# A decoder layer on one core: the stage of cross values and feed-forward in another order

## Chip, core and metric

The kernel runs on one core of a Trainium2 chip. The metric is the device time of one execution in microseconds (us). Engines are named as in the profile: PE (TensorE), DVE (VectorE), ACT (ScalarE), POOL (GpSimd), SP (the queue that issues the DMAs). Each engine works through its own instructions in the order in which the program issued them; an instruction that waits holds back everything queued behind it on its engine.

## What is computed

One decoder layer over 8 sequences of 128 tokens and 512 features, in float32. Three blocks follow each other; each adds to x, and a layernorm (no gain, no bias) follows each:

```python
x = _layernorm(x + attn(x))            # causal self-attention, 32 heads, 4-bit weights
x = _layernorm(x + xattn(x, ctx, ctx)) # cross-attention, 16 heads of 32
x = _layernorm(x + ffn(x))
```

In the cross-attention the softmax runs over the axis of sequence and head, not over the keys (`softmax(scores, axis=0)` with scores of shape (8*16, 128, 128)). So each weight needs the sum over all sequences, and each sequence's exponentials can only be weighed at the end. The feed-forward is

```python
h = relu(layernorm(xf @ gw1.T + gb1) * gamma + beta)   # gate, 32 wide
gates = h @ gw2.T + gb2                                # 8 experts, top 2
main = xf @ weight.T                                   # 512 x 512
tmp = einsum('ni,eir->enr', xf, lora_A)                # 8 x 16, weighed by the gate
out = main + einsum('enr,ero->no', tmp * w, lora_B) / 16
```

with a limit on how many tokens an expert may take over all 1024 tokens, so that the expert part is finished only when all tokens have passed the gate.

## The kernel before

The first 620 us or so are the self-attention, the cross projections and the cross scores. Then comes the stage that the change touches, a loop over the sequences i = 0 to 7 in which TensorE works on three sequences at once. What one round issues, and in which order, is written out by hand in a string, `AV_SEQ` (L62); each letter is one step (`step`, L1294), and letters without a meaning do nothing:

- A, `cross_values(i)` (L1251): 16 heads times (values x weighed exponentials), 32 matmuls into the bank "sc", copied by ACT to `avs`.
- B, `cross_residual(i)` (L1268): four transposes of `avs` on PE (tr_av), DVE adds them to the residual `acc`, then `normalised` (L214): bn_stats and bn_aggr on DVE, then three small operations on POOL (the add of epsilon, L199; the power, L200; the negated mean times that, L211).
- L: ACT applies the normalisation of sequence i-1 in place (L218).
- X, `turn_x2(i-1)` (L1090): four transposes of the normalised x (tr_x), copied by ACT to `x2f`.
- P, `gate_in(i-1)` (L1095): x times the gate's first layer and lora_A together (pg, 160 columns), ACT copies the lora part to `tmp` (L1099), DVE adds gb1 to make `h` (L1101), then `normalised` for h, as above.
- N: ACT applies the oldest waiting normalisation of h (L218).
- f: the next quarter of the main product of sequence i-2 (L1111): one 128x512 float32 product, which the trace shows as two matmuls. Up to four are waiting per round; what the letters don't take is issued at the round's end.
- W: one of four weighings (`weigh`, L1080): exponentials of four heads times the inverse sum, 128x512, in place. By `WEIGH_ON = 'vvgg'` the first two of a round run on DVE, the others on POOL.
- E (rounds 5, 6, 7): ACT moves a finished main product from its bank to `acc`.
- G, H, h in round 5 and J, K in round 7: the gate's second layer. G and J transpose h of several sequences and ACT applies relu (L1122, L1123); H and K multiply by gw2 (pgate, L1130); h is one of two halves of the top-2 choice on DVE (L1141 on), 11 small operations. The first group (sequences 0 to 3) has its transposes and pgate in the bank "tr", which X uses too; the second (4, 5) in "sc", which A uses.

At the start of round 4 thirteen memsets and two small POOL operations, and three small ones on DVE, prepare tables for the gate (L1324 to L1338). Before the loop the exponentials of sequences 0 and 1 are weighed (L1217 to L1224); in the loop, round i weighs sequence i+1. After the loop a second string, `END_SEQ`, orders the rest: the four quarters for sequence 6, then X for sequence 7, and everything up to the output.

Of the kernel before, what the change touches and what calls it, by code (L numbers as in the profile page):

```python
# [10 lines left out]
F32 = mybir.dt.float32  # L11
# [4 lines left out]
ALU = mybir.AluOpType  # L16
# [3 lines left out]
P = 128  # L20
B, S, D = 8, 128, 512
# [12 lines left out]
EPS = 1e-5  # L34
# [24 lines left out]
WEIGH1_ON = 'vvgg'  # L59
LADD_AT = 4  # L60
GSUM_ON = 'g'
AV_SEQ = 'LNEvvWWfvfAvWXJWffBdfKPGdffHhfffhff'  # L62
GATES = ((0, 4, 'tr'), (4, 2, 'sc'), (6, 1, 'po'), (7, 1, 'tr'))
GATE_IN = 5
LATE_SOFT = 6
# [75 lines left out]
def decoder_kernel(ctx: ExitStack, tc: tile.TileContext, a: dict, out: bass.AP):  # L141
    nc = tc.nc

    const = ctx.enter_context(tc.tile_pool(name="const", bufs=1))
    stat = ctx.enter_context(tc.tile_pool(name="stat", bufs=4))
# [25 lines left out]
    minus_half = const.tile([P, 1], F32, name="minus_half")  # L171
# [15 lines left out]
    def statistics(x, name, wait=0, aggregations=None):  # L187

        st = stat.tile([P, 6], F32, tag="bn", name=f"bn_{name}")
        nc.vector.bn_stats(st[:], x)  # L190
        mv = stat.tile([P, 2], F32, tag="mv", name=f"mv_{name}")
        if aggregations is None:
            nc.vector.bn_aggr(mv[:], st[:])
        else:
            aggregations.append(lambda: nc.vector.bn_aggr(mv[:], st[:]))
        rstd = stat.tile([P, 1], F32, tag="rstd", name=f"rstd_{name}")

        def power():
            nc.gpsimd.tensor_scalar(rstd[:], mv[:, 1:2], EPS, None, ALU.add)  # L199
            nc.gpsimd.tensor_tensor(rstd[:], rstd[:], minus_half[:], ALU.pow)  # L200

        if aggregations is None:
            later(wait, power)
        else:
            aggregations.append(power)
        return mv, rstd

    def negated(mv, rstd, name):

        nmr = stat.tile([P, 1], F32, tag="nmr", name=f"nmr_{name}")  # L210
        nc.gpsimd.tensor_scalar(nmr[:], mv[:, 0:1], rstd[:], -1.0, ALU.mult, ALU.mult)  # L211
        return nmr

    def normalised(x, name):  # L214

        mv, rstd = statistics(x, name)
        nmr = negated(mv, rstd, name)
        return lambda: nc.scalar.activation(x, x, AF.Identity, scale=rstd[:], bias=nmr[:])  # L218

    def layernorm(dst, t, tag, wait=0):  # L220
# [8 lines left out]
    def later(n, f, projects=False):  # L229

        if slot[0] == 0 or n == 0:
            return f()
        delayed.append((slot[0] + n, f, projects))
# [609 lines left out]
    def chunk(hf, m, rg):  # L843
        return (hf * KT + m) * 4 + rg
# [28 lines left out]
    def group_of(c):  # L873
        return next(i for i in range(GROUPS) if c < FIRST[i + 1])

    def max_of(gi):
        return gmax[:, gi, :] if gi < EARLY else lmax[:, gi - EARLY + 1, :]
# [20 lines left out]
    def across(x, n=HALF):  # L898
        return x.unsqueeze(1).to_broadcast([P, n, S])
# [180 lines left out]
    def weigh(b, m, engine):  # L1080
        hf, j = divmod(b, HALF)
        c, end = chunk(hf, m, 0), chunk(hf, m, 0) + 4
        while c < end:
            gi = group_of(c)
            n = min(end, FIRST[gi + 1]) - c
            e = quads[c // 4][:, c % 4 : c % 4 + n, j, :]
            engine.tensor_tensor(e, e, across(max_of(gi), n), ALU.mult)  # L1087
            c += n

    def turn_x2(t):  # L1090
        tr = transposed(bank("tr", f"tr_x2{t}", (P, KT, S)), t)
        x2f[t] = fp.tile([P, KT, S], F32, tag="x2f", name=f"x2f{t}", bufs=3)
        nc.scalar.copy(x2f[t][:], tr[:])

    def gate_in(t):  # L1095
        ps = bank("av", f"pg{t}", (P, FW - D))
        for kt in range(KT):
            nc.tensor.matmul(ps[:], x2f[t][:, kt, :], fg[:, kt, :], start=(kt == 0), stop=(kt == KT - 1))
        nc.scalar.copy(tmp[:, t, :], ps[:, :P])  # L1099
        ht = h[:, t, :]  # L1100
        nc.vector.tensor_tensor(ht, ps[:, P:], rows["gb1"][:], ALU.add)  # L1101
        return normalised(ht, f"g{t}")
# [112 lines left out]
    def engine_of(m, on=WEIGH_ON):  # L1215
        return nc.vector if on[m] == "v" else nc.gpsimd
# [34 lines left out]
    def cross_values(i):  # L1251

        av = bank("sc", f"xav{i}", (P, KT, S))
        hf, j = divmod(i, HALF)
        for k in range(XH):
            m, g = divmod(k, 4)
            nc.tensor.matmul(
                av[ts(g, XD), m, :],
                values_of(i)[:, ts(k, XD)],
                scores_of(chunk(hf, m, g))[:, j, :],  # L1260
                start=True,
                stop=True,
                tile_position=(0, g * XD),
            )
        avs[i] = fwp.tile([P, KT, S], F32, tag="raw", name=f"avs{i}", bufs=KT)
        nc.scalar.copy(avs[i][:], av[:])

    def cross_residual(i):  # L1268
        tr = bank("po", f"tr_av{i}", (P, KT, S))
        for m in range(KT):  # L1270
            nc.tensor.transpose(tr[:, m, :], avs[i][:, m, :], ident[:])
        res = acc[:, i, :].rearrange("p (d h) -> p d h", h=XH)
        nc.vector.tensor_tensor(
            res, res, tr[:].rearrange("p m (g d) -> p d m g", g=4).rearrange("p d m g -> p d (m g)"), ALU.add
        )
        apply[i] = normalised(acc[:, i, :], f"x{i}")

    def evacuate(t):
        if EVACUATE_ON == "a":
            nc.scalar.copy(acc[:, t, :], outp.pop(t)[:])  # L1280
        else:
            nc.vector.tensor_copy(acc[:, t, :], outp.pop(t)[:])

    def gate(k, what):

        t, n, tag = GATES[k]
        if what == "G":
            gate_turn(t, n, tag)
        elif what == "H":
            pg[k] = gate_top(t, n, gate_out(t, n, tag))  # L1290
        else:
            pg[k].pop(0)()

    def step(what, i, state):  # L1294
        if what == "L" and i - 1 in apply:
            apply.pop(i - 1)()
        elif what == "W" and 0 < i + 1 < B and i:
            m = state["w"] = state.get("w", -1) + 1
            weigh(i + 1, m, engine_of(m))
        elif what == "A" and i < B:  # L1300
            cross_values(i)
        elif what == "B" and i < B:
            cross_residual(i)
        elif what == "X" and i:
            turn_x2(i - 1)
        elif what == "P" and i:
            norm[i - 1] = gate_in(i - 1)
        elif what == "N" and norm:
            norm.pop(min(norm))()
        elif what in "GHh" and i == GATE_IN:  # L1310
            gate(0, what)
        elif what in "JK" and i == B - 1:
            gate(1, "GH"["JK".index(what)])
        elif what == "E" and i in EVACUATE:
            evacuate(EVACUATE.index(i))
        elif what == "f" and fill:
            fill.pop(0)()

    for i in range(B):
        if i == 0:  # L1320
            f_cm = open_ffn()
        if i == GATE_IN - 1:
            for e in range(NE):
                nc.gpsimd.memset(rank[:, e : e + 1], float(NE - e))  # L1324
            nc.gpsimd.memset(ones[:], 1.0)
            nc.gpsimd.memset(minus_one[:], -1.0)
            for k in range(TOPK):
                nc.gpsimd.memset(orders[1][:, k, :], float(k))

            nc.vector.tensor_reduce(  # L1330
                experts[:, 0], ident[:].rearrange("p (e r) -> p e r", r=R), AX.X, ALU.add
            )
            nc.gpsimd.tensor_scalar(experts[:, 1], experts[:, 0], ALPHA, None, ALU.mult)
            nc.gpsimd.tensor_copy(experts[:, 0], experts[:, 1])
            of, other = (rank[:].unsqueeze(i).to_broadcast([P, NE, NE]) for i in (2, 1))
            nc.vector.tensor_tensor(orders[0][:, :, 0, :], other, of, ALU.is_lt)
            nc.vector.tensor_tensor(orders[0][:, :, 1, :], other, of, ALU.is_gt)
            nc.gpsimd.memset(hT[GH : GH + 1], 1.0)  # L1338
        state = {}
        for what in AV_SEQ:  # L1340
            step(what, i, state)
        while fill:
            fill.pop(0)()
        if i:
            fill.extend(main_product(i - 1, "proj"))
# [256 lines left out]
```

## Time and profile before

| | |
|---|---|
| median of 3 runs | 737.8 us (736.91 to 738.52) |
| profiled execution | 737.73 us |
| its span, first to last instruction | 735.9 us |
| mean granted PE clock over the span | 0.976 |
| loop of this stage, B of sequence 0 to X of sequence 7 | 639.70 to 702.66 us |

The profiled execution lies 1.83 us above its span and 0.07 us below the median. Rows of the timeline read: start, duration (both us), engine, line, operation, output<-input, shape, count; in brackets the idle time just ahead of it and who ended it. Starts of PE's transposes in the loop, by sequence:

| sequence | B (tr_av) | X (tr_x) |
|---|---|---|
| 0 | 639.70 | 645.82 |
| 1 | 646.73 | 652.62 |
| 2 | 654.83 | 659.90 |
| 3 | 662.12 | 666.76 |
| 4 | 668.97 | 675.50 |
| 5 | 679.32 | 686.31 |
| 6 | 688.52 | 693.16 |
| 7 | 696.97 | 702.66 |

### The profile page before, as it was taken

The page shows a single profiled execution, that of the slowest core. Times are in us where ns is not written, and L with a number is a line of the kernel's source. Part 1 is how long each engine was busy: PE and PEld are TensorE (multiplying, and loading weights), DVE is VectorE, ACT ScalarE, POOL GpSimd, SP SyncE. Part 2 cuts the span into 40 slices and gives each one's busy share as a digit, 9 for nine tenths or more (in the row PEclk, how much of TensorE's full clock was granted, in tenths as well). Part 3 has the DMA queues.
Part 4 walks back from the last instruction along what each step waited for, and adds up shares of the span by engine and source line. Part 5 has one row for each costly group of instructions (what it writes and reads, how often), then busy time and mean ns, then how long its engine had stood idle before and what let it go on. Part 6 is the DMA issues. An engine that isn't in the chain of part 4 may idle for free. (4 is left out here: it accounts for less than half of the span.)

```text
span 735.9 us, 12053 instructions
## 1 busy us (share of the span) xinstructions
PE 687.3 (93%) x3762; PEld 545.7 (74%) x3762; DVE 622.2 (85%) x1448; ACT 376.1 (51%) x1018; POOL 443.9 (60%) x434
## 2 busy tenths in 40 slices
PE   7899999999999999999999999999999898488875
PEld 4687788888888888888888888877887666355542
DVE  5989999999999999999999999998444989934555
ACT  4465655555565555465465554547524554132433
POOL 3764756667576775766758666577503566377325
PEclk9999999999999999999999999999999999689987
DMA  8778342443443343343343332163001001100003
GB/s 285 213 198 254 102 110 69 129 106 82 122 122 87 87 121 96 85 128 103 87 108 73 82 88 61 30 185 115 1 1 29 1 1 60 32 1 1 1 1 114
DMA packets 36242, 65.73 MB, mean 89 GB/s; under 512 B 5327, under 2 KB 7503, under 8 KB 36178
## 3 DMA queue, kind: packets, MB, share of 16 engines
q1 hardware_dynamic: 36178, 64.96, 32.0%
q8 instruction: 30, 0.49, 0.3%
q14 instruction: 34, 0.28, 0.1%
HBM read 41.87 MB, written 2.10 MB: 60 GB/s over the span
## 5 line engine op out<-in xcount | busy, mean ns | idle before, releaser
L392 ACT ACTIVATE p<-p,nmx 128x128 f32<-128x128 f32 x256 | 99.8, 391 | 88.8 <-DVE nmx L383 88.8
L310 PE MATMUL ps<-xh,w 128*128 128x512 f32 x336 | 140.8, 419 | 0.4 <-DVE part L320 0.4
L310 PE MATMUL ps<-xl,w 128*128 128x512 f32 x336 | 132.0, 393 | 0.0
L399 POOL TENSOR_TENSOR p<-p,rden 128x512 f32<-128x512 f32 x64 | 68.1, 1064 | 102.6 <-DVE rden L398 79.3
L320 DVE SCALAR_TENSOR_TENSOR part<-ps,scales,part 128x512 f32<-128x512 f32 x168 | 124.8, 743 | 2.0 <-PE ps L310 0.4
L344 POOL TENSOR_TENSOR sw<-sw,tables 128x512 f32<-128x512 f32 x71 | 92.7, 1306 | 50.4 <-DMA sw<-x 34.7
L345 POOL TENSOR_TENSOR q<-t,sw 128x512 f32<-128x512 f32 x62 | 93.6, 1510 | 10.0 <-DVE sw L344 5.0
L343 DVE TENSOR_TENSOR t<-x,tables 128x512 f32<-128x512 f32 x80 | 78.4, 980 | 0.7 <-POOL q L345 0.7
L378 PEld LDWEIGHTS sc<-k,q 128*128 128x128 f32 x512 | 67.0, 191 | 8.4 <-DVE q L345 2.1
L435 PE MATMUL po<-woh,ch 128*128 128x512 f32 x256 | 72.2, 403 | 0.0
L316 ACT ACTIVATE part<-ps,scales 128x512 f32<-128x512 f32 x84 | 57.8, 689 | 28.0 <-PE ps L310 28.0
L310 PEld LDWEIGHTS ps<-xh,w 128*128 128x128 f32 x336 | 63.3, 188 | 11.3 <-DVE part L320 0.6
L310 PEld LDWEIGHTS ps<-xl,w 128*128 128x128 f32 x336 | 63.7, 190 | 10.3
L378 PE MATMUL sc<-k,q 128*128 128x128 f32 x512 | 68.2, 275 | 2.5 <-DVE q L345 1.9
L435 PE MATMUL po<-woh,cl 128*128 128x512 f32 x256 | 69.4, 393 | 0.0
L435 PE MATMUL po<-wol,ch 128*128 128x512 f32 x256 | 69.4, 393 | 0.0
L184 ACT CAST ph<-tr 128x512 fp32r<-128x512 f32 x64 | 37.4, 584 | 53.7 <-PE tr L409 53.5
L383 DVE CUSTOM_DVE_ANT_0 p<-sc,causal 128x128 f32<-128x128 f32 x256 | 58.4, 283 | 0.3 <-PE sc L378 0.3
L320 DVE SCALAR_TENSOR_TENSOR x<-ps,scales,part 128x512 f32<-128x512 f32 x70 | 52.4, 749 | 5.5 <-PE ps L310 0.5
L435 PEld LDWEIGHTS po<-wol,ch 128*128 128x128 f32 x256 | 48.2, 188 | 10.9
L435 PEld LDWEIGHTS po<-woh,cl 128*128 128x128 f32 x256 | 48.1, 188 | 10.8
L435 PEld LDWEIGHTS po<-woh,ch 128*128 128x128 f32 x256 | 45.8, 189 | 8.4
(259 smaller groups left out, 1475.8 us busy)
## 6 DMA issues: line engine op xcount, KB each, us to landing
sw<-x SPq DMA_DIRECT2D x160, 128.0 KB, 2.3
raw<-in_qkv SPq DMA_DIRECT2D x28, 384.0 KB, 3.6
oraw<-in_qw_o SPq DMA_DIRECT2D x32, 256.0 KB, 2.8
osc<-in_scales_o SPq DMA_DIRECT2D x32, 256.0 KB, 3.7
xraw<-in_xT SPq DMA_DIRECT2D x4, 512.0 KB, 5.8
acc<-in_x SPq DMA_DIRECT2D x8, 256.0 KB, 5.4
ctxraw<-in_ctxT SPq DMA_DIRECT2D x2, 1024.0 KB, 7.1
out<-o SPq DMA_DIRECT2D x8, 256.0 KB, 2.0
```

Source lines behind the costliest of these rows:

```text
L184: nc.scalar.copy(hi, src)
L310: nc.tensor.matmul(ps[:], w[:, kt, ts(j, HD)], x[:, kt, ts(hf, HN)], start=(i == 0), stop=(i == 1))
L316: nc.scalar.activation(p[:], ps[:], AF.Copy, scale=sc)
L320: nc.vector.scalar_tensor_tensor(to, ps[:], sc, parts[0][:], ALU.mult, ALU.add)
L343: later(delay("cos"), lambda: engine("cos").tensor_tensor(seqs(t[:]), seqs(x[:]), table(cos_t[m]), ALU.mult), True)
L344: later(delay("sin"), lambda: engine("sin").tensor_tensor(seqs(sw[:]), seqs(sw[:]), table(sin_t[m]), ALU.mult), True)
L345: later(delay("q"), lambda: engine("q").tensor_tensor(dst, t[:], sw[:], ALU.add), True)
L378: nc.tensor.matmul(sc[:, r, :], t["q"][:, r, ts(j, S)], t["k"][:, ts(j, S)], start=True, stop=True)
L383: nc.vector.tensor_tensor_reduce(out=p[:, r, :], in0=sc[:, r, :], in1=causal[:], scale=-1.0, scalar=3e38, op0=ALU.add, op1=ALU.min, accum_ ...
L392: nc.scalar.activation(p[:, r, :], p[:, r, :], AF.Exp, scale=-1.0, bias=nmx[:, r : r + 1], accum_out=den[:, r : r + 1],)
L399: nc.gpsimd.tensor_tensor(p[:], p[:], rden[:].unsqueeze(2).to_broadcast([P, REP, S]), ALU.mult)
L435: nc.tensor.matmul(po[0][:], c[:, r, :], w[:, r, :], start=(r == 0 and i == 0), stop=(r == REP - 1 and i == 2))
```

## The change

Three edits. The order string is rewritten; a round weighs the sequence two ahead (rounds 0 to 5) instead of one ahead (rounds 1 to 6); and `normalised` does the add of epsilon on DVE instead of POOL.

```diff
-AV_SEQ = 'LNEvvWWfvfAvWXJWffBdfKPGdffHhfffhff'
+AV_SEQ = 'LENAXJfBWWfKffPWWGHhh'
...
     def normalised(x, name):
 
-        mv, rstd = statistics(x, name)
-        nmr = negated(mv, rstd, name)
+        st = stat.tile([P, 6], F32, tag="bn", name=f"bn_{name}")
+        nc.vector.bn_stats(st[:], x)
+        mv = stat.tile([P, 2], F32, tag="mv", name=f"mv_{name}")
+        nc.vector.bn_aggr(mv[:], st[:])
+        rstd = stat.tile([P, 1], F32, tag="rstd", name=f"rstd_{name}")
+        nc.vector.tensor_scalar(rstd[:], mv[:, 1:2], EPS, None, ALU.add)
+        nc.gpsimd.tensor_tensor(rstd[:], rstd[:], minus_half[:], ALU.pow)
+        nmr = stat.tile([P, 1], F32, tag="nmr", name=f"nmr_{name}")
+        nc.gpsimd.tensor_scalar(nmr[:], mv[:, 0:1], rstd[:], -1.0, ALU.mult, ALU.mult)
         return lambda: nc.scalar.activation(x, x, AF.Identity, scale=rstd[:], bias=nmr[:])
...
-        elif what == "W" and 0 < i + 1 < B and i:
+        elif what == "W" and i + 2 < B:
             m = state["w"] = state.get("w", -1) + 1
-            weigh(i + 1, m, engine_of(m))
+            weigh(i + 2, m, engine_of(m))
```

Without the letters that do nothing, and with f where four are waiting, a round on PE changes from

```
f f A(i) X(i-1) f f B(i) P(i-1)      main product of i-2
```

to

```
A(i) X(i-1) f B(i) f f f P(i-1)      main product of i-2
```

On DVE a round was: weighing pair, residual and statistics of x(i), h and its statistics. It becomes: residual and statistics of x(i), weighing pair, h and its statistics. On POOL the weighing pair moves from the round's start to its end, behind the operations of both statistics. On ACT the copy of `tmp` in a round keeps its place ahead of the next round's L; E moves ahead of N; N stays ahead of the copies of `avs` and `x2f`. In round 7, K (pgate of sequences 4 and 5) stays behind B and comes ahead of the last two f and P. DMAs and their order are the same.

More of the change, by code (lines that the diff above doesn't have):

```diff
@@ L206, in statistics, with normalised @@
         return mv, rstd
-    def negated(mv, rstd, name):
+    def normalised(x, name):
+        st = stat.tile([P, 6], F32, tag="bn", name=f"bn_{name}")
[5 more added lines that the diff above has]
+        nc.gpsimd.tensor_tensor(rstd[:], rstd[:], minus_half[:], ALU.pow)
         nmr = stat.tile([P, 1], F32, tag="nmr", name=f"nmr_{name}")
         nc.gpsimd.tensor_scalar(nmr[:], mv[:, 0:1], rstd[:], -1.0, ALU.mult, ALU.mult)
-        return nmr
-    def normalised(x, name):
-        mv, rstd = statistics(x, name)
-        nmr = negated(mv, rstd, name)
         return lambda: nc.scalar.activation(x, x, AF.Identity, scale=rstd[:], bias=nmr[:])
```

## The prediction

> **What bounds the kernel now.** I read the page first, then the waits of the stage from 625 to 700 us, then its timeline engine by engine, because the changed order only exists there: up to 640 us the two orders issue the same work, and from the last transposes of x (702.66 us) they do so again.
>
> ```profile
> PE 687.3 (93%) x3762; PEld 545.7 (74%) x3762; DVE 622.2 (85%) x1448; ACT 376.1 (51%) x1018; POOL 443.9 (60%) x434
> PEclk9999999999999999999999999999999999689987
> ```
>
> PE is busy 93% of the whole span, but the last slices, this stage, are its weakest, and there its clock is not full. The stage's waits (who, for whom, us in total, times, longest):
>
> ```profile
> ACT acc L218 <- POOL nmr_x L211: 17.5, 7, 5.3
> PE tr_x L819 <- ACT acc L218: 6.4, 6, 2.9
> PE xav L1257 <- DVE E L1087: 5.9, 2, 4.6
> ACT h L218 <- POOL nmr_g L211: 3.0, 6, 0.5
> ```
>
> PE waits for a weighing (DVE E) only twice, both for sequence 0, which neither order moves. What PE waits for later is the layernorm of x: six times, 6.4 us. The timeline of PE over one undisturbed round, and the one disturbed round:
>
> ```profile
> 659.90 0.66 PE L819 MATMUL tr_x<-ident,acc 128*128 128x128 f32 x4 [0.66 <-ACT acc L218]
> 660.40 1.88 PE L1111 MATMUL pf<-fw,x2f 128*128 128x512 f32 x4
> 662.12 0.60 PE L1271 MATMUL tr_av<-ident,avs 128*128 128x128 f32 x4
> 662.55 1.25 PE L1098 MATMUL pg<-fg,x2f 128*128 128x160 f32 x8
> 663.64 1.88 PE L1111 MATMUL pf<-fw,x2f 128*128 128x512 f32 x4
> 665.45 1.08 PE L1257 MATMUL xav<-E,xv 128*32 128x128 f32 x32
> ...
> 675.50 0.66 PE L819 MATMUL tr_x<-ident,acc 128*128 128x128 f32 x4 [2.11 <-ACT acc L218]
> 676.00 3.54 PE L1111 MATMUL pf<-fw,x2f 128*128 128x512 f32 x4
> ```
>
> Start to start, a round costs PE: X (tr_x) 0.50, one f (two matmuls, half of a pf row) 0.86, B (tr_av) 0.43, P (pg) 1.09, A (xav) 1.08; with four f 6.54 us. The rounds took 7.29 and 6.85 us (B at 654.83, 662.12, 668.97). The last row ran at half clock after PE had stood for 2.11 us. On ACT:
>
> ```profile
> 659.04 0.81 ACT L218 ACTIVATE acc<-acc,nmr_x,rstd_x 128x512 f32<-128x512 f32 x1 [2.21 <-POOL nmr_x L211]
> 660.36 0.41 ACT L218 ACTIVATE h<-h,nmr_g,rstd_g 128x32 f32<-128x32 f32 x1 [0.51 <-POOL nmr_g L211]
> 660.68 0.56 ACT L1266 COPY avs<-xav 128x512 f32<-128x512 f32 x1
> 661.15 0.59 ACT L1093 COPY x2f<-tr_x 128x512 f32<-128x512 f32 x1
> ```
>
> N (the gate's normalisation, row two) stands ahead of the copy of avs that B needs. Today it costs 0.51 us of ACT and no PE time: B comes at 662.12, over 0.8 us after that copy.
>
> **What the change does.** [...] No matmul, transpose, copy or DMA is added; SP's queue is untouched.
>
> *The loop through x becomes shorter.* B(i), residual, statistics, normalise, X(i), then B(i+1) after one f instead of two: 0.86 us less.
>
> *The add of epsilon goes from POOL (0.22) to DVE* (nearest row: the 128x6 add at L1198, 0.17). Sixteen times 0.17 on DVE; each chain gains about 0.1 us (POOL's add to its power 0.31 us; DVE's add follows the aggregate by 0.21, the power that by about 0.31 instead of 0.30). From below: nothing gained, if DVE is late.
>
> *The weighing pair on DVE moves* to just behind the statistics of x, the POOL pair behind those of the gate. DVE's pair now runs against POOL's power and nmr of the same x. The row that shows this price: nmr_x at 658.17 took 0.83 us beside the DVE pair of 657.61 to 658.87, and 0.27 at 665.59 without. The Trainium skill (SBUF — State Buffer, "Who interferes with whom") says that a DVE instruction with two SBUF inputs and a GpSimd instruction that reads SBUF lock each other out for the whole instruction, whichever is first. The trace agrees for POOL; but DVE's pair took 1.26 us although POOL's power was already running at 657.50, so I charge POOL alone. By the rule DVE's pair would start up to 0.6 us later, which matters in two rounds (gate statistics queued behind the pair): at most +1.2 us. I take 0.
>
> *P comes after all four f, and that is the new danger.* The gate statistics start 2.58 us later relative to B than now, but N keeps its place ahead of the avs copy. From B(i) to B(i+1) through the gate, each step with a row: B 0.43; three f 2.58; P to its copy tmp 1.29 (655.27 to 656.56); to h on DVE 0.30; to bn 0.22; to aggregate 0.30; to the new add 0.21; to POOL's power 0.31; to nmr 0.67; to N on ACT 0.30; to the avs copy 0.32; to B(i+1) 0.64 (639.06 to 639.70). Sum 7.57 us. Through x it is: tmp stands ahead of x's normalise on ACT, so that begins at 0.43+2.58+1.29+0.17 = 4.47, X at 5.34, f, B(i+1) at 6.70. PE alone: 6.54. So the gate sets the round, 7.57. Queued behind N are the copies of avs and x2f, and B waits for the first.
>
> Now the stage, B to B, measured and forecast:
>
> B1 to B2: 8.10. POOL's nmr for x1 is held to the end of the DVE pair (add 2.76 after B1, pair until 4.1), X(1) at about 5.2, and the gate statistics queue behind that pair: N at 6.1, avs 6.5, B2 at 7.1. So −1.0.
> B2 to B3 and B3 to B4: 7.29 and 6.85 become 7.57: +0.3, +0.7.
> B4 to B5: 10.35, of which the half clock costs 1.7 (3.54 against 1.88). Now the thirteen memsets and small POOL operations (2.94 us, 667.12 to 670.06) come behind POOL's pair for sequence 5, which ends 1.5 after B4; the DVE tables wait for them, so residual 4 starts at 2.2 instead of 0.6. POOL's power starts at 4.45, nmr ends at 5.35, X(4) comes at 6.3. Gate: h behind DVE's pair at 5.2, N 7.2, B5 8.2. So −2.15, if PE's idle (about 1.1) doesn't drop the clock.
> B5 to B6: 9.20. P, gate transposes, relu, pgate as now, at 6.54; A to 7.6. X(5) needs the bank of pgate, free only after six steps of the top-2 on DVE. They begin at 6.65; two have both inputs in SBUF and meet POOL's pair for sequence 7 (6.6 to 9.1): nearest row, the onehot at 684.39 with 1.27 for 0.19 us. They end at 9.5, X(5) at 9.6, B6 at 10.95: +1.75. Without the collision 8.1 and 9.45: from +0.25 to +1.75; I take the upper because 684.39 shows it.
> B6 to B7: 8.45. As 7.57, but the gate transposes behind X(6) use the bank of xav(7) and wait for the avs copy: 6.93+0.56, then 0.39 and one f: 8.8: +0.35.
> B7 to X(7): 5.69. Now seven f lie there instead of four: B 0.43, seven f 6.02, pgate 0.55, P 1.09 = 8.1: +2.4.
>
> Sum +2.35. Ahead of B1: POOL's add and power at 643.03 took 0.57 and 0.86 against the DVE pair; one of them goes: −0.4. At the end, the same chain for token tile 7 (709.63 to 711.80) gains about 0.15. Total +1.8 us. The work behind X(7), 33.2 us, is unchanged. Span 735.9+1.8 = 737.7; the profiled execution took 737.73, 1.83 outside the span, so 739.5 (the median of the runs, 737.8, is 0.1 above it).
>
> **The clock.** The Trainium skill (TensorE: Matmul & The Clock Gate, "What's actually happening") ties the drop to half clock to an idle window of about 3.4 us. By that rule none of my stalls (1.1 at X(4), 2.0 at X(5), 1.5 at the gate transposes) drops it: 739.5. But the row above dropped after 2.11 us, while gaps of 1.3 us and less did not; by the row X(5) may drop it and cost another 1.7: 741.2. I keep 739.5 as likeliest, since the clock must fall in a window that also holds four f.
>
> **Rivals.**
> *One (faster): the gate doesn't hold B.* If N is ready before the avs copy is due, PE sets the round. For it: six waits for N total only 3.0 us now. Against: P moves back by 2.58 us and N doesn't. It decides from 1.0 us (7.57−6.54): were the gate chain that much shorter. Then the rounds give −1.6, −0.75, −0.3, −2.7, +1.75, −1.4, +2.4 = −2.6, with start and end −3.15: 734.6 (733.1 without the collision at X(5)).
> *Two (no change): the top-2 misses POOL's pair.* −1.5: 738.0. For it: an offset of 1 us between DVE and POOL suffices.
> *Three (slower): a second slow clock,* at X(5), also at X(4) or behind B1, where PE would stand about 1 to 2 us: 741.2 to 743.
> *Four: weighing further ahead does nothing by itself.* The waits say so (both PE waits are for sequence 0); it is part of the forecast, and only the POOL and DVE collisions move.
>
> **How the numbers follow.** Forecast 0.45 (739.5; own range 738.2 to 741); slow clock 0.20; no collision 0.15; gate not binding 0.20. A measurement of this kernel tells apart about 0.2%, 1.5 us. Faster by more: nearly all of rival one, 0.18. Slower by more: 0.38 of the forecast, all of three, a little of two: 0.61. The rest, 0.21, is the same. The range reaches from 735.5 (most of rival one's way) to 743 (the upper slow clock).
>
> **What would show it.** B to B near 7.6 us between B2 and B4, with ACT's h ending the wait ahead of the avs copy and "PE tr_av <- ACT avs" as a new wait of 0.5 to 1 us; X(5) held by DVE; no 2.11 us wait at X(4); B7 to X(7) at about 8.1. Wrong if these rounds take 6.6 us, or if POOL's power in the gate chain meets DVE's pair (then longer still).

## The result and the profile after

The changed kernel takes 739.93 us (median of 9 runs, 737.04 to 741.57), the kernel before in the same comparison 736.63 us (9 runs, 734.52 to 738.52): ratio 1.0045, 95% interval 1.0026 to 1.0064, some 3 us slower. Measured again beside other runs of the kernel before (e8 below) the ratio is 1.0039 (1.0026 to 1.0052). The profiled execution took 739.79 us with a span of 738.0 us.

The page of the changed kernel, the same two rows:

```profile
PE 685.6 (93%) x3762; PEld 544.5 (74%) x3762; DVE 624.5 (85%) x1464; ACT 375.8 (51%) x1018; POOL 437.9 (59%) x418
PEclk9999999999999999999999999999999999589998
```

Sixteen adds have gone from POOL to DVE; the same matmuls run. From the waits of the stage, 625 to 703 us (who, for whom, us in total, times, longest; the lines of the code have moved by one):

```profile
ACT acc L219 <- POOL nmr_x L218: 6.7, 3, 4.9
PE xav L1258 <- DVE E L1088: 5.9, 2, 4.6
PE tr_x L820 <- ACT acc L219: 4.5, 3, 2.4
ACT h L219 <- POOL nmr_g L218: 4.5, 5, 1.3
PE tr_av L1272 <- ACT avs L1267: 2.3, 4, 0.8
PE tr_x L820 <- DVE second L1154: 1.7, 1, 1.7
PE trh L1123 <- ACT avs L1267: 1.5, 1, 1.5
```

The wait for the layernorm of x has shrunk (6.4 us in six to 4.5 us in three). The two waits for weighings are as they were: both belong to sequence 0. New are three of PE's four waits for the copy of avs ahead of tr_av (the one at sequence 0 was there) and its wait for the top-2; the one ahead of the gate transposes (trh) was 1.2 us before. One round of PE in the changed kernel's timeline:

```profile
660.65 0.66 PE L820 MATMUL tr_x<-ident,acc 128*128 128x128 f32 x4
661.14 1.02 PE L1112 MATMUL pf<-fw,x2f 128*128 128x512 f32 x2
662.85 0.66 PE L1272 MATMUL tr_av<-ident,avs 128*128 128x128 f32 x4 [0.68 <-ACT avs L1267]
663.34 2.74 PE L1112 MATMUL pf<-fw,x2f 128*128 128x512 f32 x6
665.92 1.25 PE L1099 MATMUL pg<-fg,x2f 128*128 128x160 f32 x8
667.10 1.08 PE L1258 MATMUL xav<-E,xv 128*32 128x128 f32 x32
```

and ACT at the same time:

```profile
659.78 0.81 ACT L219 ACTIVATE acc<-acc,nmr_x,rstd_x 128x512 f32<-128x512 f32 x1
661.91 0.41 ACT L219 ACTIVATE h<-h,nmr_g,rstd_g 128x32 f32<-128x32 f32 x1 [1.31 <-POOL nmr_g L218]
662.23 0.56 ACT L1267 COPY avs<-xav 128x512 f32<-128x512 f32 x1
```

and the gate's chain between the two, on DVE and POOL:

```profile
659.92 0.19 DVE L1102 TENSOR_TENSOR h<-pg,row_gb 128x32 f32<-128x32 f32 x1 [0.94 <-ACT tmp_hT L1100]
660.97 0.55 POOL L216 TENSOR_TENSOR rstd_g<-rstd_g,minus_half 128x1 f32<-128x1 f32 x1 [1.82 <-DVE rstd_g L215]
661.61 0.27 POOL L218 TENSOR_SCALAR nmr_g<-mv_g,rstd_g 128x1 f32<-128x1 f32 x1
```

X comes without a wait in this round. B is late: its input, xav, was complete at 660.59, but the copy started at 662.23, behind the gate's normalisation, for which ACT waited 1.31 us. DVE and POOL waited too, each for the step ahead of it, and the first step, P, had come behind all four f. B to B in us, from the starts of tr_av in each profile (e8 is the changed kernel again, e9 and e10 the kernel before):

| | B0-B1 | B1-B2 | B2-B3 | B3-B4 | B4-B5 | B5-B6 | B6-B7 | B7-X(7) | B0-X(7) |
|---|---|---|---|---|---|---|---|---|---|
| before, first profile | 7.03 | 8.10 | 7.29 | 6.85 | 10.35 | 9.20 | 8.45 | 5.69 | 62.96 |
| before, e9 | 7.02 | 8.50 | 7.22 | 6.85 | 8.73 | 9.11 | 8.43 | 5.69 | 61.55 |
| before, e10 | 7.03 | 8.62 | 7.22 | 6.85 | 8.74 | 9.11 | 8.43 | 5.70 | 61.70 |
| changed | 6.61 | 6.82 | 7.59 | 7.58 | 7.80 | 10.74 | 8.62 | 8.27 | 64.03 |
| changed, e8 | 6.62 | 6.83 | 7.59 | 7.58 | 7.81 | 10.75 | 8.62 | 8.27 | 64.07 |
| forecast | 6.6 | 7.1 | 7.57 | 7.57 | 8.2 | 10.95 | 8.8 | 8.1 | 64.9 |

### The profile page after: what moved, and what is told of

Its sections match the earlier page's. It is cut to its first block, busy times and chain, and to the rows that moved or that the text cites. A ratio compares the mean times of both kernels' runs of the same rounds, so it can differ in the third digit from the quotient of the medians.

```text
span 738.0 us, 12049 instructions
## 1 busy us (share of the span) xinstructions
PE 685.6 (93%) x3762; PEld 544.5 (74%) x3762; DVE 624.5 (85%) x1464; ACT 375.8 (51%) x1018; POOL 437.9 (59%) x418
## 4 chain that ended last, share of the span: by engine, by line
PE 73%; DVE 13%; DMA 4%; POOL 3%; ACT 3%; issue 3%; SPq 1%; DVEq 0%; POOLq 0%; ACTq 0%
PE po L436 22%; PE ps L311 20%; PE sc L379 7%; PE av L421 6%; PE tr L410 3%; PE pxk L659 3%; PE pf L1112 3%; PE pxv L623 2%; DMA sw<-x 2%; DVE top L935 2%; PE pxq L659 2%; DVE E L946 1%; DMA xwrawk<-in_WkT 1%; PE xsc L916 1%; DVE E L1088 1%
```

## The experiments

Each ratio is to runs of the kernel before on the same chip. Theory G: the gate's normalisation, queued on ACT ahead of the avs copy, sets the round. Theory X: the chain through x, or DVE and POOL meeting, sets it.

**e1: N behind the avs copy.**

```diff
-AV_SEQ = 'LENAXJfBWWfKffPWWGHhh'
+AV_SEQ = 'LEANXJfBWWfKffPWWGHhh'
```

> The changed kernel with one letter moved: on ACT the gate's normalisation (N) stands behind the copy of avs instead of ahead of it. Theory G (the gate chain, through N, holds the avs copy and so B): rounds B2 to B3 and B3 to B4 fall from 7.6 to 6.7 us (then the chain through x sets them), the wait of PE for the avs copy ahead of tr_av goes, the wait ahead of the gate transposes of sequences 4 and 5 (1.53 us) goes too; 2 to 3 us faster than the changed kernel. Theory X (the longer rounds come from the chain through x or from DVE and POOL meeting): rounds stay near 7.6 us and the time within 0.5 us of the changed kernel.

Ratio 1.0017 (0.9991 to 1.0042). B2 to B3 and B3 to B4: 6.69 and 6.68 us; B0 to X(7) 61.85. ACT, then PE, of this kernel's timeline:

```profile
657.12 0.59 ACT L1267 COPY avs<-xav 128x512 f32<-128x512 f32 x1
658.37 0.41 ACT L219 ACTIVATE h<-h,nmr_g,rstd_g 128x32 f32<-128x32 f32 x1 [0.66 <-POOL nmr_g L218]
```

```profile
658.47 0.60 PE L1272 MATMUL tr_av<-ident,avs 128*128 128x128 f32 x4
```

N still waits for POOL, but now behind the copy, and tr_av starts without a wait. One letter takes 0.9 us from each such round: theory G. The wait ahead of the second gate transposes, which was to go, fell from 1.53 us to two of 0.30 and 0.48 us (the second transpose waits for h itself). By the ratios the kernel is some 2 us faster than the changed one, but its twelve runs spread from 735.5 to 744.3 us and the intervals overlap; the rounds carry the verdict, not the total.

**e2: P ahead of the last three f.**

```diff
-AV_SEQ = 'LENAXJfBWWfKffPWWGHhh'
+AV_SEQ = 'LENAXJfBWWPfKffWWGHhh'
```

> The changed kernel with P moved ahead of the last three f of a round instead of behind them. Theory G: the statistics of the gate begin about 2.6 us earlier, N is ready when the avs copy is due, rounds of 6.6 to 6.7 us in place of 7.6, B7 to X(7) unchanged within 0.3; 3 to 4 us faster than the changed kernel. Theory X: rounds stay near 7.6.

Ratio 1.0005 (0.9989 to 1.0020). The rounds took 6.71 and 6.57 us, with N ahead of the copy as in the changed kernel: what counts is when the gate statistics are ready. By the ratios the kernel is 2.5 to 3 us faster than the changed one, a little under the 3 to 4 expected. In this execution PE's clock then fell to half; from the stretches of this profile:

```profile
680.00:682.00 2.00, 1.91 (x40) 1.78 (x40) 0.78 (x3) 1.43 (x3) 2.00 (x2) 1.00 0.00 0
682.00:684.00 2.00, 1.01 (x12) 0.92 (x6) 1.73 (x9) 0.58 (x1) 0.25 (x1) 0.56 0.00 0
686.00:688.00 2.00, 2.00 (x10) 2.00 (x9) 1.16 (x2) 0.00 (x0) 0.00 (x0) 0.50 0.00 0
```

The third number from the right is the granted clock. B5 to B6 took 11.42 us, and B0 to X(7) 62.93 in place of the 3 us or more below 64 that I estimate for the rounds at full clock.

**e3: the add alone.** The kernel before with only the new `normalised`.

> The kernel before with only the add of epsilon moved from POOL to DVE in normalised. By the sum of the prediction 0.1 us per chain, 0.4 at sequence 0: B0 to X(7) shorter by 0.3 to 1.0 us against the kernel before, and the half clock in round 4 may or may not remain (1.7 us). If instead the add on DVE is what lengthens the rounds of the changed kernel, rounds B2 to B4 are longer here too, by 0.3 us or more.

Ratio 0.9974 (0.9956 to 0.9991): faster than the kernel before by about 1.9 us. B0 to X(7) 60.59 us, 1.0 below e9 and e10; B0 to B1 6.61 as forecast; PE's wait in round 4 was 1.06 us instead of 2.1. B2 to B3 was 0.4 us longer, B3 to B4 0.15 shorter. The two together are 0.25 us longer where the changed kernel's are 1.1, so the add is not what costs there.

**e4: round 5 weighs on DVE alone.**

```diff
-            weigh(i + 2, m, engine_of(m))
+            weigh(i + 2, m, nc.vector if i == GATE_IN else engine_of(m))
```

> The changed kernel with all four weighings of round 5 on DVE, so that POOL reads nothing while the top-2 of the first gate group runs. If POOL's pair for sequence 7 holds the top-2 and so the bank for X(5): the wait of PE ahead of tr_x in that round (1.67 us) falls to 0.5 or less, B5 to B6 from 10.7 to 9.4 to 9.6, 1.0 to 1.3 us faster than the changed kernel. If the top-2 is slow by itself: B5 to B6 stays at 10.5 or more.

Ratio 1.0002 (0.9988 to 1.0016). PE ahead of X(5), first in the changed kernel, then in e4:

```profile
687.65 0.63 PE L820 MATMUL tr_x<-ident,acc 128*128 128x128 f32 x4 [1.67 <-DVE second L1154]
```

```profile
685.78 0.63 PE L820 MATMUL tr_x<-ident,acc 128*128 128x128 f32 x4 [0.48 <-DVE second L1154]
```

and the fifth step of the top-2 on DVE, in the same order:

```profile
686.31 0.96 DVE L1152 TENSOR_TENSOR onehot<-onehot,gfirst 128x32 f32<-128x32 f32 x1
```

```profile
685.22 0.19 DVE L1152 TENSOR_TENSOR onehot<-onehot,gfirst 128x32 f32<-128x32 f32 x1
```

The same instruction takes 0.96 us beside POOL's pair (684.73 to 687.2) and 0.19 without; the third step, which also reads two inputs from SBUF, takes 0.60 and 0.19. B5 to B6 fell from 10.74 to 9.56, everything else stayed within 0.03. The collision costs 1.2 us. By the ratios this kernel is about 3 us faster than the changed one, more than the 1.2 us that the stage shows; where the rest comes from isn't shown.

**e5: the waits found so far taken away.**

```diff
-AV_SEQ = 'LENAXJfBWWfKffPWWGHhh'
+AV_SEQ = 'LENAXfJBWWPfGKffHhhWW'
...
-            weigh(i + 2, m, engine_of(m))
+            weigh(i + 2, m, nc.vector if i == GATE_IN else engine_of(m))
...
-        if i == GATE_IN - 1:
+        if i == 1:
             for e in range(NE):
```

> The changed kernel with each wait found so far taken away: P ahead of the last three f, the gate transposes of the first group two steps earlier, those of the second group behind one f, the top-2 ahead of the weighings that are left, round 5 weighing on DVE alone, and the tables of round 4 prepared in round 1. Theory G with the collision at X(5): rounds of 6.6 to 6.8 us from B1 to B5, B5 to B6 near 8, B6 to B7 near 7.3, B7 to X(7) 8.3; B0 to X(7) near 57 us where the changed kernel had 64.0, so 5 to 7 us faster than it and 3 to 5 faster than the kernel before. If PE is slowed by its clock or by something else in these rounds, B0 to X(7) stays above 60 us.

732.77 us (731.71 to 734.26) against 738.37: ratio 0.9925 (0.9912 to 0.9938), by the ratios 5.5 us faster than the kernel before and 8.5 faster than the changed one, more than expected. B to B: 6.62, 6.91, 6.72, 6.56, 6.72, 8.57, 6.77, then 8.27; B0 to X(7) 57.14, as expected. A round of its timeline has no wait left:

```profile
658.47 1.08 PE L1258 MATMUL xav<-E,xv 128*32 128x128 f32 x32
659.48 0.66 PE L820 MATMUL tr_x<-ident,acc 128*128 128x128 f32 x4
659.97 1.02 PE L1112 MATMUL pf<-fw,x2f 128*128 128x512 f32 x2
660.84 0.60 PE L1272 MATMUL tr_av<-ident,avs 128*128 128x128 f32 x4
```

**e6: the new order, weighing one ahead.**

```diff
-        elif what == "W" and i + 2 < B:
+        elif what == "W" and 0 < i + 1 < B and i:
...
-            weigh(i + 2, m, engine_of(m))
+            weigh(i + 1, m, engine_of(m))
```

> The changed kernel weighing one sequence ahead again (rounds 1 to 6), with its new order kept. If the second sequence ahead is what makes this order possible: POOL's pair, now behind the gate statistics, ends some 9 us after B, A of the next round waits for it, rounds B1 to B7 become about 10 to 11 us, 10 to 20 us slower than the changed kernel, and PE waits for weighings in every round. If weighing further ahead does nothing: within 1 us of the changed kernel.

769.69 us, ratio 1.0428 (1.0409 to 1.0447): 29 us slower than the changed kernel by the ratios where 10 to 20 were expected, with rounds of 11.5 to 14.1 us instead of 10 to 11. PE in one round:

```profile
666.85 0.66 PE L1258 MATMUL xav<-E,xv 128*32 128x128 f32 x8 [2.99 <-POOL E L1088]
668.07 0.66 PE L1258 MATMUL xav<-E,xv 128*32 128x128 f32 x8 [0.57 <-POOL E L1088]
668.65 1.12 PE L820 MATMUL tr_x<-ident,acc 128*128 128x128 f32 x4
669.56 1.91 PE L1112 MATMUL pf<-fw,x2f 128*128 128x512 f32 x2
```

A waits for each half of POOL's pair, and with such a wait the clock halves (tr_x 1.12 for 0.66, one f 1.91 for 1.02), for 6.83 us at a time, about half of each round from the second on. The expectation left that out.

**e7: order and weighing alone**, with the add back on POOL (the old `normalised`).

> The changed kernel with the add of epsilon back on POOL: order and weighing two ahead alone. By the prediction each chain is 0.05 to 0.1 us longer: rounds B2 to B4 of 7.6 to 7.7 us, B0 to B1 7.0 instead of 6.6; 0.5 to 1.5 us slower than the changed kernel in B0 to X(7). If the add did more than that (the kernel before gained about 2 us from it): 2 us or more slower.

Ratio 1.0084 (1.0066 to 1.0102). Rounds of 7.73 us, 0.15 longer than in the changed kernel where 0.05 to 0.1 was expected; B0 to B1 7.02, 0.4 longer as expected. But B0 to X(7) was 66.90, 2.8 above the changed kernel where 0.5 to 1.5 was expected; about 1.3 of that (12.15 from B5 to B6 for 10.74, less the longer chain) comes with a stretch at half clock from 688.9 to 692.3, which began in a wait of 1.81 us at X(5). By the ratios the add is worth some 3 us here and 2 in e3, more than the sum of the chains; the intervals are wide (0.7 to 3.2 us in e3), and where the rest lies isn't shown.

**e8: the changed kernel again.**

> The changed kernel once more, on the chip of the others and against the same runs of the kernel before. Waits are set by the order, so B-to-B times agree with the first profile within 0.1 us wherever the clock is full; a slow stretch of the clock may fall elsewhere in the stage and cost 1 to 3 us. Against the kernel before: slower by 0 to 0.6%.

Ratio 1.0039 (1.0026 to 1.0052); every B to B within 0.02 us of the first profile (table above). No stretch at half clock in the stage behind 651.5 us, as in the first.

**e9 and e10: the kernel before again.**

> The kernel before, profiled a second time. Its first profile has B0 to X(7) at 62.96 us with about 1.7 us of half clock in round 4, the changed kernel 64.0 without any, which is less than the distance of the medians (about 3 us). If the half clock in round 4 is an accident of that execution: B4 to B5 is 8.6 here instead of 10.35, B0 to X(7) near 61.2, and the distance in the stage is 2.8 us. If it follows from PE's 2.11 us wait each time: B4 to B5 is 10.3 again, and the rest of the distance lies outside the stage.

> The kernel before, a third profile, with the same two readings as the second: B4 to B5 near 8.6 where the clock holds, near 10.3 where it drops; all other B-to-B times within 0.1 us of the first profile where the clock is full.

Ratios 1.0005 (0.9988 to 1.0021) and 0.9995 (0.9981 to 1.0009). Round 4 in e9, the rows that stood in the prediction with 2.11 and 3.54:

```profile
677.14 0.65 PE L819 MATMUL tr_x<-ident,acc 128*128 128x128 f32 x4 [2.10 <-ACT acc L218]
677.63 1.88 PE L1111 MATMUL pf<-fw,x2f 128*128 128x512 f32 x4
```

The same wait, and the clock holds. B4 to B5 is 8.73 and 8.74 in these two, 10.35 in the first.

**e11: the kernel before with the tables in round 1.**

```diff
-        if i == GATE_IN - 1:
+        if i == 1:
             for e in range(NE):
```

> The kernel before with the gate's tables prepared in round 1 instead of round 4, nothing else. If PE's 2.11 us wait in round 4 comes from POOL's 2.9 us of memsets ahead of the statistics: the wait falls below 0.5, B4 to B5 to about 7 us with a full clock, 1.5 us faster than the kernel before, 3.2 where that one drops its clock; round 1 up to 0.5 us longer. If the wait stays at 1.5 or more, it is POOL's weighing pair that holds the statistics.

Ratio 0.9980 (0.9965 to 0.9996). PE's wait in round 4 fell from 2.1 to 0.75, not below 0.5, and B4 to B5 to 7.38; B0 to B1 was 0.6 shorter too. B1 to B2 rose to 9.32 and B3 to B4 to 7.41, so that B0 to X(7) gained only 0.6 to 0.7 us: most of it was given back.

## Why the prediction was right, and where its sum was off

The time and the direction came as forecast (739.5 against 739.93, slower), by the forecast's mechanism; one term of the sum was mis-sized, and the sum's 1.8 us is less than the distance of the medians, 3.3 us. That the two times lie only 0.4 us apart is in part luck: the sum began at 737.73 us, 1.1 above the median of the nine runs beside which the changed kernel was measured.

*The gate sets the round, 7.57.* Measured 7.59 and 7.58, twice. e1 and e2 take the two ends of that chain apart (N's place, P's place), and either one brings 6.6 to 6.7. Rival one (PE sets the round) falls as a forecast and holds as a limit: the combined kernel comes close to it, with rounds of 6.56 to 6.72 from B2 to B5 for a PE cost of 6.54. Its 3 us of gain were too many: e1 and e2, which free B from the gate, are level with the kernel before; its sum too was taken from the 10.35 us of B4 to B5 (below).

*The first rounds.* B0 to B1 −0.42 for −0.4. B1 to B2 6.82 for 7.1.

*X(5) and the top-2.* 10.74 for 10.95, with the collision that I took. e4 removes it for 1.2 us; rival two's 1.5 was a little high. The Trainium skill's rule of the shared pair (SBUF — State Buffer, "Who interferes with whom") holds for these two DVE instructions: both were issued behind a weighing of POOL, and each ended within 0.1 us after it.

*B6 to B7, B7 to X(7).* 8.62 and 8.27 for 8.8 and 8.1. The 2.6 us more in the last stretch are no new work: three f have moved there, out of the stretch from B1 to B2.

*B4 to B5: the term that was mis-sized, "So −2.15".* The 8.2 was near (7.80; the memsets took 2.1 us, not 2.9, because two small POOL operations no longer met a DVE pair: 0.25 and 0.19 us for 0.77 and 0.48). The 10.35 from which it was taken was not typical: 1.6 of it was a stretch at half clock that e9 and e10 don't have. Against those the round gains 0.93, not 2.55. The stage is then 64.03 and 64.07 against 61.55 and 61.70, +2.3 to +2.5 us, and the sum of the prediction, corrected in this one term, +3.0 (1.8, with 7.80 − 8.73 = −0.93 in place of −2.15).

*Start and end of the execution.* Not foreseen, and outside the change: ahead of the stage the eight matmuls of the last sum ran at half clock in both profiles of the changed kernel (2.08 us for 1.16), and behind X(7) the clock came back sooner (32.14 us to the end, 33.2 in the three profiles of the kernel before). The two nearly cancel. The 0.15 us forecast for token tile 7 came to about 0.05 (PE waits there for 2.38 us instead of 2.43). The slow sum came in e2 too (2.08) and in no other kernel with the new order; PE had stood 3.15 to 3.74 us ahead of it in these three profiles and 0.9 to 2.3 in the others. The code there is the same in all, so the change doesn't make it; why both profiles of the changed kernel share it isn't settled.

*The clock.* Rival three didn't come about in either profile of the changed kernel, with waits of up to 1.67 us at full clock. My row of 2.11 us is too simple, and so is the Trainium skill's rule of an idle window of about 3.4 us (TensorE: Matmul & The Clock Gate, "What's actually happening") when it is read as a gap of that length: the clock held after 2.10 and 2.11 us (e9, e10), and fell in a wait of 1.81 (e7) and in e2, where no wait at full clock exceeded 1 us. But that section also calls the window free-running, and there the traces agree. In all thirteen profiles every stretch at half clock whose two ends are in the profile lasts a whole multiple of 3.41 us, and in one execution all the ends lie on one grid of 3.41 us, which lies elsewhere in the next. A slot is one step of this grid. Here are two neighbouring slots around the wait in round 4, in the first profile of the kernel before, then in e9, whose grid is counted on from the ends of its own slow stretches (stretch, its length, busy time of PE and number of its instructions, the same of PEld, DVE, ACT and POOL; third from the right the granted clock):

```profile
672.67:676.08 3.41, 1.30 (x33) 1.03 (x25) 1.13 (x2) 0.95 (x2) 2.89 (x7) 1.00 0.00 0
676.08:679.49 3.41, 3.41 (x6) 1.24 (x5) 0.00 (x0) 1.72 (x4) 2.27 (x2) 0.50 0.00 0
```

```profile
672.28:675.69 3.41, 2.76 (x37) 1.25 (x35) 3.06 (x7) 0.27 (x1) 3.24 (x4) 1.00 0.00 0
675.69:679.11 3.42, 1.97 (x8) 1.19 (x9) 0.00 (x0) 2.36 (x5) 3.05 (x7) 1.00 0.00 0
```

In the first profile the whole wait (673.39 to 675.50) falls into one slot, PE is busy for 1.30 us of it (38%), and the next slot runs at half clock. In e9 an edge at 675.69 divides the wait, as one at 676.25 does in e10, and the clock holds. Over the thirteen profiles, each of the 46 slots at full clock with PE busy for less than 44% was followed by one at half clock, and none of the 2468 with 70% or more. In between both happened: in the slot with the wait at X(5), PE was busy for 51% in the changed kernel and the clock held, for 53% in e7 and it fell; in e2 it fell behind a slot with 69%. What decides there isn't shown. So it was in part luck that rival three stayed away, and my reason against it fails: the slot of that wait (684.81 to 688.22) did not hold four f; the first f began at 688.11. The gap of 1.3 us that I called harmless (1.34, ahead of 637.43) stood in a stretch already at half clock.

*Weighing two ahead.* Rival four is half right. PE's only two waits for weighings, both for sequence 0, are as they were; but e6 shows that the new order, with POOL's pair behind the gate statistics, costs 29 us without it. Weighing two ahead in the old order, and E ahead of N, were not run alone.

So the stage's +2.4 us can be put together from the runs: the gate, which begins 2.6 us later and keeps its place in ACT's queue, 2.2 (64.03 − 61.85, e1); the collision at X(5) 1.2 (e4); the add −1.0 (e3). That leaves about nothing for the shorter chain through x and the three f that moved behind B7. Neither was run alone, and gains measured in different kernels need not add up.

## What to carry to other kernels

When a step is moved back in one engine's order, follow its result to the next instruction that waits for it, and look at what is queued behind that instruction: here a 0.4 us normalisation of a side branch held the copy on the main chain, and one letter moved the round from 7.6 to 6.7 us. Add up a loop separately for each chain that closes it, and move consumer and producer together. Before a difference is taken from one profile, split off the stretches of slow clock, since they may not come again.

## What the hardware showed beyond expectation

A stretch at half clock doesn't follow from the length of one PE wait: 2.1 us led to it in one of three executions of the same kernel, the one in which the whole wait fell into one slot of a grid of 3.41 us. In e6, with waits of 3 us in each round, it came every round from the second on, and the rounds took 13 us where my estimate at full clock had 10 to 11. Where the clock is full, B to B repeats within 0.1 us between executions of a kernel (0.01 in the two of the changed kernel), while the total spreads by 4 to 4.6 us.
